# First rows of x ahead of the weights, a longer assumed time for early loads, and a new table of rules, in a planned three-part layer kernel

## The chip, the cores and the metric

The kernel runs on one core of one Trainium2 chip. The metric is the device time of one execution in microseconds (us); lower is better. A core has five engines that each work through a queue of their own in order: TensorE (PE, its weight loads PEld), VectorE (DVE), ScalarE (ACT), GpSimd (POOL) and SyncE (SP), which issues all the transfers of this kernel.

## The reference

The input x has 8 sequences of 1024 tokens with 256 channels. Four residual steps follow one another, each on the layer norm of what came before:

```
x = x + A(layernorm(x))     # A: x' + retention(x'), 4 heads, q/k width 64, v width 128, rotary, gated
x = x + F(layernorm(x))     # F: channel mix: sigmoid(xr @ W_r) * (relu(xk @ W_k)**2 @ W_v),
                            #    xr, xk mixed with the token before
x = x + Battn(layernorm(x)) # Battn: softmax attention, 16 heads of 16, a bias by relative distance
x = x + F(layernorm(x))
```

## The kernel before, in words

**The work.** Everything is done per sequence b (`for b in range(B)`). `retention(b)` handles step A in chunks of 256 tokens (`prepare`: load of the rows and their statistics; `turn_chunk`: normalising to z, transposing, and making nT, which is split into two parts so that fast matmuls keep their precision) and then blocks of 128 tokens (`queries_keys`, `values`, `gates`, `scores`, `attend`, `state`, `output`; their PSUM tiles are qps, vps, gps, aps, ops, sps, wps; the running state is S). `ffn_front` is step F (tiles ftp, kps, rps, yps). `project_b` makes queries and keys of step Battn and stores them in DRAM (stk, vd); `maxima` computes all scores once for the row maxima (PSUM tile p, maxima in pm); `weigh` computes them again (tile s), takes exponentials (e) and sums them with the values (tile acc); `back` projects (bop) and does the last step F.

**Forms of matmul.** p and s use half of the array's rows, so two matmuls, one for each of two heads, run as a pair side by side. acc uses four column strips of the array. Nearly all others use the whole array. The planner calls these forms modes.

**The order.** The program is first recorded as a list of operations (`Plan.record`), each with an engine, a planned cost, a tail (the time until its result can be used) and a target. `Plan.issue` then plays it through on a clock of its own: at each moment each engine takes, of the operations that are ready and have a free buffer, the one with the lowest key, and the instructions are written out in that order. On the chip each engine follows this written order and waits where the data is not there yet. For a load the cost is 0.4 and the tail 2.0 plus bytes/100000, in us.

**The table.** On PE the key is the target plus additions that a rule gives: `change` (a charge for changing the mode), `least` (how many PSUM slots must be free before PE changes over to p or s), `pairs` (how many sums of acc should be ready before PE changes over to them) and four offsets for other operations, p, s and acc. There are 16 rules (`RULES`). `TURNS` is a string of 122 hexadecimal digits; digit i names the rule for the i-th stretch of 20 us of the planner's clock, and the last one holds to the end:

```
rule = RULES[int(TURNS[min(int(now / STRETCH), len(TURNS) - 1)], 16)]
```

**The start.** Targets of the loads are -1.1 for the constants (cm), the norm's weights (ln) and the first weight (`split(wqk, ...)`: four loads of 128 KB, Wq and Wk in two halves; ACT casts each half and DVE subtracts the cast from it for a second part). The first sequence's `retention` starts at -1.0, and `next_ones` (Wv, Wg, wo_a) stands just after its first steps. `later()` at -0.9 loads everything else: the weights of F and of Battn, bqk, rel, the bias table, `stk` rows of statistics (two DRAM to DRAM copies of 1 MB), and small tables from which DVE works out the factors (tiles d, db, fac, then 16 times kr, each of which two stores carry to stk; kr shares five buffers with other tiles). Of equal targets the one recorded first goes first.

Of the kernel before, what the change touches and what calls it, by code (L numbers as in the profile page):

```python
# [10 lines left out]
F32 = mybir.dt.float32  # L11
# [8 lines left out]
P = 128  # L20
# [3 lines left out]
HALF = 512  # L24
# [17 lines left out]
NC, CT = 4, 2 * P  # L42
# [34 lines left out]

STRETCH = 20
TURNS = (
    "00070270877472bf8931ef967bfe1d0522ff04383dfe37be3f1f7ef668e19e9c33271224f3e73df5"  # L80
    "5663e6176b19fd77763fbb3cafd79ff9fb9bf84111"
)
SWITCH = 0.1

# [227 lines left out]
class Plan:  # L312
# [66 lines left out]
    def record(self, eng, real, method, args, kw):  # L379
        cost = kw.pop("cost", None)  # L380
        views = [a for a in list(args) + list(kw.values()) if isinstance(a, View)]
        outs = [kw[k] for k in ("out", "accum_out") if isinstance(kw.get(k), View)]
        if "out" not in kw and isinstance(args[0], View):
            outs.append(args[0])
        if method in ("matmul", "transpose"):
            out, group = outs[0].t, kw.pop("group", None)
            op = self.last
            if op is None or op.group is not group or group is None and op.out[0] is not out:
                op = self.new(eng)
                op.out, op.cost, op.group = [], 0.0, group  # L390
                self.last = op
                k, m = args[1].shape[0], 1
                for n in args[1].shape[1:]:
                    m *= n
                op.mode = ("rows" if k == 64 and m == P else "cols") if k == 64 or m == 64 else "all"
                if out.tag == "acc":
                    op.mode = "acc"
                op.late = (0.055 if method == "transpose" else 0.1) if op.mode == "all" else 0.0
            if out not in op.out:
                op.out.append(out)  # L400
            op.cost += cost
        else:
            op = self.new(eng)
            n = 1
            for v in views:
                m = 1
                for d in v.shape[1:]:
                    m *= d
                n = max(n, m)
            if method == "dma_start":  # L410
                size = 4
                for d in (args[0] if isinstance(args[0], View) else views[0]).shape:
                    size *= d
                op.cost, op.tail = 0.4, 2.0 + size / 100000.0
            else:
                op.cost = self.estimate(eng, method, n, views, {
                    **kw, "op": args[3] if len(args) > 3 else None,
                    "scalar": len(args) > 2 and isinstance(args[2], View),
                })
                op.tail = AFTER[eng]  # L420
        op.calls.append((real, method, args, kw))
        for v in views:
            if v.t.space != "in":
                self.touch(op, v, any(v is o for o in outs))
        return op
# [186 lines left out]
def layer_kernel(ctx: ExitStack, tc: tile.TileContext, ap: dict, out: bass.AP):  # L612
    nc = tc.nc
    x = ap["x"]
# [9 lines left out]
    plan = Plan(ctx, tc)  # L624
    plan.target = -1.1
    act, dve, pool, sp = (plan.engine(n, e) for n, e in (
        ("ACT", nc.scalar), ("DVE", nc.vector), ("POOL", nc.gpsimd), ("SP", nc.sync)))
    pe = plan.engine("PE", nc.tensor)

    def const(shape, name, dt=F32):  # L630
        return plan.tile(shape, dt, name, name, 1)

    def tile2k(tag, bufs=1, dt=F32):
        return plan.tile([P, HALF], dt, tag, tag, bufs)
# [37 lines left out]
    def split(w, names):  # L672
        for c in range(ND):
            t = tile2k(f"xo{c % 2}", 2)
            for s, k in enumerate(names):
                n = 2 * D // len(names)
                sp.dma_start(t[:, s * n : (s + 1) * n], ap[k][c * P : (c + 1) * P])
            act.copy(w[0][:, c], t)
            dve.tensor_tensor(w[1][:, c], t, w[0][:, c], ALU.subtract)

    split(wqk, ("a_Wq", "a_Wk"))
    wo_a = const([P, RH, D], "wo_a")
    gn = const([P, 1], "gn")
# [27 lines left out]
    def small(shape, name, bufs=2, dt=F32):  # L711
        return plan.tile(shape, dt, name, name, bufs)
# [93 lines left out]
    def power(a, n, name):  # L806

        y = small([P, n], name + "_y", 4)
        pool.tensor_tensor(y, a, mhalf[:, :n], ALU.pow)

        t = small([P, n], name + "_t", 1)
        pool.tensor_tensor(t, y, y, ALU.mult)
        pool.tensor_tensor(t, t, a, ALU.mult)
        pool.tensor_scalar(t, t, -0.5, 1.5, ALU.mult, ALU.add)
        pool.tensor_tensor(y, y, t, ALU.mult)
        return y
# [7 lines left out]
    def moments(xc, name):  # L824

        st = small([P, 2, 6], name + "_st", 1)
        mv = small([P, 2, 2], name + "_mv", 4)
        for n in range(2):
            dve.bn_stats(st[:, n, :], xc[:, n, :])
            dve.bn_aggr(mv[:, n, :], st[:, n, :])  # L830
        less = mv[:, :, 0]
        pool.tensor_scalar(less, less, -1.0, 0.0, ALU.mult, ALU.add)
        return mv
# [14 lines left out]
    def product(a, b, name):  # L848
        m = small([P, 2], name, 4)
        pool.tensor_tensor(m, a, b, ALU.mult)  # L850
        return m
# [11 lines left out]
    def rows_in(ap2, c):  # L863
        return ap2[c * CT : (c + 1) * CT, :].rearrange("(n p) d -> p n d", p=P)
# [6 lines left out]
    xc = {}  # L871


    def retention(b):
        norms = {}

        def prepare(c):

            t = tile2k("xc", 4).rearrange("p (n d) -> p n d", n=2)
            sp.dma_start(t, rows_in(x[b], c))  # L880
            xc[b, c] = t
            mv = moments(t, "a")


            a = small([P, 4], "a_a", 1)
            pool.tensor_scalar(a[:, 2:4], mv[:, :, 1], 1.0 + EPS, EPS * EPS, ALU.mult, ALU.add)
            pool.tensor_scalar(a[:, 0:2], mv[:, :, 1], 1.0, EPS, ALU.mult, ALU.add)
            rs = power(a, 4, "a")
            rs1, rz = rs[:, 0:2], rs[:, 2:4]

            s1, m1 = small([P, 2], "a_s1", 4), product(mv[:, :, 0], rs1, "a_m1")
            pool.tensor_scalar(s1, rs1, 1.0, 1.0, ALU.mult, ALU.add)
            norms[c] = mv, rz, s1, m1
# [161 lines left out]
        plan.target = b - 1.0  # L1055
        S, gT = None, None
        prepare(0)
        nTs[0] = turn_chunk(0)
        tick()
# [3 lines left out]
        tick()  # L1063
        values(0)
        prepare(1)
        tick()
        qk = turned_heads(0)
# [7 lines left out]
        for n in range(NT):  # L1075
# [18 lines left out]
            if more:  # L1094
                qk = turned_heads(n + 1)
                tick()
                gates(n + 1)
                tick()
                if n % 2 == 0 and n + 2 < NT:
                    nTs[n // 2 + 1] = turn_chunk(n // 2 + 1)  # L1100
                    if n // 2 + 2 < NC:
                        prepare(n // 2 + 2)
                    tick()
                at = scores(qk)
                tick()
# [347 lines left out]
```

## Time and profile before

| | |
|---|---|
| median of 3 runs | 2548.52 us (2542.09, 2548.52, 2551.93) |
| profiled execution | 2557.27 us, span of its instructions 2555.5 us |
| granted TensorE clock, mean | 0.992 |
| PE busy | 2476.2 us (97%), 15814 matmuls |
| DVE, ACT, POOL busy | 2107.5, 2069.9, 1589.0 us |
| DMA | 251.17 MB, mean 98 GB/s |

Busy times are of one profiled execution. A timeline line reads: start, busy time, engine, line, operation, out<-in, shape, count, and in brackets how long the engine was idle before it and what ended that. Nearly all lines carry L608, where the recorded operations are written out, so tiles tell them apart. An engine name with q (SPq) is its sequencer, which issues transfers. In the table by stretches each row gives the stretch, its length, then busy time and count for PE, PEld, DVE, ACT and POOL, the granted clock, the share of DMA time and GB/s.

### The profile page before, as it was taken

Reading aid. Unit: us, or ns where it says so; the run is one execution under the profiler, and the core shown is the slowest. Engines: PE = TensorE matmul, PEld = TensorE weight load, DVE = VectorE, ACT = ScalarE, POOL = GpSimd, SP = SyncE. Lnnn points to the kernel's source line nnn. Section 1 sums busy time; section 2 is a strip of 40 time slices with the busy share of each in tenths; the row PEclk is TensorE's granted clock in tenths of the full one; section 3 lists DMA queues with packets and bytes.
Section 4 is the critical chain, followed back from the end, with each engine's and each line's share of the span. In section 5 each row is a group of like instructions: output and inputs, shape, how many; then the busy total and the mean of one; then the engine's idle time right before and its main releaser. Section 6 shows DMA issues by size and latency. Waiting matters only on the chain.

```text
span 2555.5 us, 51508 instructions
## 1 busy us (share of the span) xinstructions
PE 2476.2 (97%) x15814; PEld 1459.8 (57%) x15814; DVE 2107.5 (82%) x6230; ACT 2069.9 (81%) x5334; POOL 1589.0 (62%) x2675
## 2 busy tenths in 40 slices
PE   5999999999999999999999999999999999999997
PEld 3887755555555555555555555555555555554555
DVE  6767998888888888988888788888888888788855
ACT  3565598888989888988888789988898888688883
POOL 2467666666756666666656576666666666666642
PEclk9999999999999999999999999999999999999999
DMA  7136322444344333332324333333233344444322
GB/s 175 42 108 150 81 58 68 130 107 112 85 106 105 84 100 101 110 98 79 92 64 119 97 107 102 94 78 109 68 94 93 102 118 115 124 115 113 93 64 72
DMA packets 252224, 251.17 MB, mean 98 GB/s; under 512 B 89042, under 2 KB 226180, under 8 KB 251924
## 3 DMA queue, kind: packets, MB, share of 16 engines
q1 hardware_dynamic: 251956, 247.89, 36.6%
q8 instruction: 132, 2.16, 0.4%
q14 instruction: 136, 1.11, 0.2%
HBM read 151.32 MB, written 98.59 MB: 98 GB/s over the span
## 4 chain that ended last, share of the span: by engine, by line
PE 79%; DVE 8%; DMA 5%; ACT 3%; POOL 2%; issue 1%; SPq 1%; POOLq 0%; DVEq 0%; ACTq 0%
PE acc L608 16%; PE p L608 10%; PE s L608 10%; PE kps L608 4%; PE wps L608 4%; PE yps L608 4%; PE rps L608 4%; PE qkp L608 3%; PE vps L608 3%; PE qps L608 3%; PE gps L608 3%; PE ops L608 3%; DVE pm L608 3%; ACT e L608 2%; PE bop L608 2%
## 5 line engine op out<-in xcount | busy, mean ns | idle before, releaser
L608 DVE TENSOR_REDUCE pm<-p 128x1 f32<-128x512 f32 (+2 forms) x2048 | 1057.2, 557 | 89.7 <-PE p L608 87.9
L608 ACT ACTIVATE e<-s 128x512 f32<-128x512 f32 (+2 forms) x2048 | 1008.0, 527 | 52.8 <-PE s L608 49.3
L608 POOL TENSOR_TENSOR e<-e,hk 128x512 f32<-128x512 f32 (+1 forms) x558 | 614.0, 1107 | 348.7 <-ACT e L608 326.9
L608 PE MATMUL acc<-e,va 128*17 128x512 f32 x4096 | 529.5, 599 | 3.7 <-ACT e L608 3.4
L608 DVE CUSTOM_DVE_ANT_0 jmax<-p,hk 128x256 bf16<-128x256 f32 (+1 forms) x1152 | 427.0, 371 | 111.8 <-PE p L608 106.6
L608 ACT COPY e<-s 128x256 f32<-128x256 f32 (+1 forms) x1116 | 400.0, 358 | 82.3 <-PE s L608 80.2
L608 PE MATMUL p<-k,q 64*128 64x512 f32 x2048 | 460.4, 438 | 5.0 <-DVE pm L608 2.8
L608 PE MATMUL s<-q,k 64*128 64x512 f32 x2048 | 456.7, 436 | 5.8 <-DVE pm L608 3.2
L608 ACT ACTIVATE e<-e 128x512 f32<-128x512 f32 (+1 forms) x576 | 336.2, 586 | 59.0 <-POOL e L608 56.1
L608 PEld LDWEIGHTS p<-k,q 64*128 64x128 f32 x2048 | 207.5, 185 | 248.4 <-ACT e L608 93.7
L608 PEld LDWEIGHTS s<-q,k 64*128 64x128 f32 x2048 | 206.0, 185 | 204.6 <-issue 69.8
L608 PEld LDWEIGHTS acc<-e,va 128*17 128x17 f32 x4096 | 77.7, 95 | 189.5 <-issue 161.6
L608 PE MATMUL kps<-xk,W_k 128*128 128x256 f32 x512 | 130.8, 399 | 10.7 <-DVE xk L608 9.7
L608 PE MATMUL rps<-W_r,xr 128*128 128x256 f32 x512 | 126.8, 390 | 3.0 <-DVE pm L608 1.8
L608 PE MATMUL yps<-W_v,xk 128*128 128x256 f32 x512 | 127.2, 392 | 1.1 <-DVE pm L608 0.5
L608 PE MATMUL wps<-wo_a,gs 128*128 128x256 f32 x512 | 125.7, 388 | 0.6 <-ACT gs L608 0.5
L608 PEld LDWEIGHTS kps<-xk,W_k 128*128 128x128 f32 x512 | 95.2, 195 | 40.7 <-issue 19.3
L608 PE MATMUL qps<-wqk,nT 128*128 128x512 f32 x384 | 106.8, 413 | 7.0 <-DVE nT L608 6.6
L608 PEld LDWEIGHTS rps<-W_r,xr 128*128 128x128 f32 x512 | 93.4, 191 | 34.5 <-DVE pm L608 5.1
L608 PEld LDWEIGHTS yps<-W_v,xk 128*128 128x128 f32 x512 | 93.6, 192 | 28.7 <-issue 12.0
L608 PEld LDWEIGHTS wps<-wo_a,gs 128*128 128x128 f32 x512 | 92.5, 190 | 26.5 <-issue 4.7
L608 POOL TENSOR_TENSOR ao_y<-ao_a,mhalf 128x4 f32<-128x4 f32 x64 | 65.7, 1026 | 66.5 <-DVE ao_a L608 65.8
(185 smaller groups left out, 4175.3 us busy)
## 6 DMA issues: line engine op xcount, KB each, us to landing
stk<-qk SPq DMA_DIRECT2D x192, 256.0 KB
hk<-ud SPq DMA_DIRECT2D x128, 256.0 KB
q<-stk SPq DMA_DIRECT2D x128, 256.0 KB
k<-stk SPq DMA_DIRECT2D x128, 256.0 KB
od<-o SPq DMA_DIRECT2D x64, 256.0 KB
vd<-vst SPq DMA_DIRECT2D x64, 136.0 KB
va<-vd SPq DMA_DIRECT2D x32, 272.0 KB
xc<-in_x SPq DMA_DIRECT2D x32, 256.0 KB
```

The lines of the kernel that those rows point to most:

```text
L608: getattr(real, method)(*[be(a) for a in args], **{k: be(a) for k, a in kw.items()})
```

## The change

Three edits. The load of the first 256 rows of x (256 KB) is recorded before the first weight's loads, at target -1.1, into the same kind of buffer (xc) that `prepare` took before, and `prepare` of the first chunk uses it. The tail of a transfer that is recorded at a target below -0.85 becomes 2.0 plus bytes/50000 in the planner's clock; this takes in all loads and stores of the start, the first two chunks of x and everything in `later`. The string `TURNS` is replaced; 22 of its 122 digits are the same at the same place.

```diff
 TURNS = (
-    "00070270877472bf8931ef967bfe1d0522ff04383dfe37be3f1f7ef668e19e9c33271224f3e73df5"
-    "5663e6176b19fd77763fbb3cafd79ff9fb9bf84111"
+    "01f23221077472bf8958e587083491e68871f2b49d36a6f05684487b6ccde338cff55263777f276f"
+    "53f68b29ff7a5356f4326638b8f59ba679b7155111"
 )
...
-                op.cost, op.tail = 0.4, 2.0 + size / 100000.0
+                op.cost, op.tail = 0.4, 2.0 + size / (50000.0 if self.target < -0.85 else 100000.0)
...
+    first = plan.tile([P, HALF], F32, "xc", "xc", 4)
+    sp.dma_start(
+        first.rearrange("p (n d) -> p n d", n=2), x[0][:CT, :].rearrange("(n p) d -> p n d", p=P)
+    )
     split(wqk, ("a_Wq", "a_Wk"))
...
-            t = tile2k("xc", 4).rearrange("p (n d) -> p n d", n=2)
-            sp.dma_start(t, rows_in(x[b], c))
+            t = (first if b == c == 0 else tile2k("xc", 4)).rearrange("p (n d) -> p n d", n=2)
+            if b or c:
+                sp.dma_start(t, rows_in(x[b], c))
```

## The prediction

> **What bounds the kernel now.** First the page: busy times and the chain that ended last.
>
> ```profile
> span 2555.5 us, 51508 instructions
> ...
> PE 2476.2 (97%) x15814; PEld 1459.8 (57%) x15814; DVE 2107.5 (82%) x6230; ACT 2069.9 (81%) x5334; POOL 1589.0 (62%) x2675
> ...
> PE 79%; DVE 8%; DMA 5%; ACT 3%; POOL 2%; issue 1%; SPq 1%; POOLq 0%; DVEq 0%; ACTq 0%
> ```
>
> TensorE sets the end; only 79 us of the span are without a matmul. The table of busy times by 80 us stretches tells where these lie (second number: PE busy).
>
> ```profile
> 0.00:80.00 80.00, 48.31 (x272) 36.08 (x273) 52.34 (x120) 35.81 (x76) 26.11 (x79) 0.96 0.58 140
> ...
> 2480.00:2555.00 75.00, 61.64 (x310) 42.80 (x302) 39.20 (x91) 32.68 (x69) 24.03 (x59) 0.95 0.24 72
> sum 2555.00, PE 2476.16 PEld 1459.77 DVE 2107.54 ACT 2069.91 POOL 1588.98; mean PE 77.38 PEld 45.62 DVE 65.86 ACT 64.68 POOL 49.66
> ```
>
> PE is idle for 31.7 us in the first 80 us, 13.4 us in the last 75, and 33.8 us in all the 2400 us between. So a better start is worth at most about 30 us. The timeline of the start shows what it waits for.
>
> ```profile
> 3.60 0.43 SPq L608 DMA_DIRECT2D xc<-in_x  x1
> ...
> 9.33 0.75 DVE L608 BATCH_NORM_STATS2 a_st<-xc 128x6 f32<-128x256 f32 x2 [1.33 <-DMA xc<-in_x]
> ...
> 15.49 0.62 ACT L608 CAST wg_a<-xo 128x512 fp32r<-128x512 f32 x1 [4.16 <-DMA xo<-in_a_Wg]
> ...
> 17.36 1.09 ACT L608 ACTIVATE z<-xc,a_nb,a_y 128x256 f32<-128x256 f32 x2
> ...
> 26.49 0.16 DVE L608 TENSOR_TENSOR d<-d,d 16x16 f32<-16x16 f32 x1 [6.09 <-DMA d<-in_b_rel]
> ...
> 29.59 0.67 DVE L608 TENSOR_TENSOR nT<-z,nT 128x512 fp32r<-128x512 f32 x1
> 30.31 2.21 PEld L608 LDWEIGHTS qps<-wqk,nT 128*128 128x128 f32 x6 [7.88 <-DVE nT L608]
> ```
>
> The first rows land at 9.33, but the first real matmul (qps) runs at 30.31. It waits for one subtraction (nT) whose inputs ACT had ready at 22.4. That subtraction stands in VectorE's queue behind an instruction on a table of bias differences, d, whose 1 KB load landed only at 26.49. So the first rows' load is not the last thing that the start waits for. A second stall follows, again in VectorE's queue.
>
> ```profile
> 49.80 0.74 DVE L608 TENSOR_SCALAR kr<-stat,fac 16x1024 f32<-16x1024 f32 x1 [0.84 <-DMA stk<-kr]
> ...
> 51.43 1.23 PE L608 MATMUL ops<-S,qkT 64*128 64x128 f32 x8 [5.25 <-ACT S L608]
> ```
>
> Here the state S sits behind kr, which waits until an earlier kr has been stored. Last, PE in the steady part, where the table of rules works.
>
> ```profile
> 1000.60 1.91 PE L608 MATMUL acc<-e,va 128*17 128x512 f32 x16
> 1002.44 0.50 PE L608 MATMUL s<-q,k 64*128 64x512 f32 x2
> ...
> 1005.29 0.50 PE L608 MATMUL p<-k,q 64*128 64x512 f32 x2
> 1005.63 0.39 PE L608 MATMUL s<-q,k 64*128 64x512 f32 x2
> 1005.86 0.39 PE L608 MATMUL p<-k,q 64*128 64x512 f32 x2
> 1006.18 1.05 PE L608 MATMUL acc<-e,va 128*17 128x512 f32 x8
> 1007.16 1.99 PE L608 MATMUL wps<-wo_a,gs 128*128 128x256 f32 x8
> ```
>
> Read the starts. Three pairs of score matmuls (half the array's rows each) take 0.89 us before acc begins; the step between the later pairs is 0.23, so a run costs 3 x 0.23 and about 0.20 once. Over the whole trace, runs of one, two and three pairs take 0.430, 0.662 and 0.895 us (medians): 0.198 per run and 0.2325 per pair. For acc, 16 matmuls take 1.84 and 8 take 0.98: 0.86 per eight and 0.12 per run. I count 873 runs of row pairs and 429 of acc, so 173 + 54 = 227 us go to changes of form that PE's busy time does not show as idle. This is what the table can move: 64 runs of pairs more or fewer are 12.7 us, 0.5% of the time and about what a measurement of this kernel can tell from no change.
>
> **The first load moved up.** No instruction, byte or buffer is added; one load goes from seventh to third in SP's queue and passes four weight loads of 128 KB. It would issue at 1.70 instead of 3.60 (third place), and four weight loads issue 0.47 us later each. What follows goes by the order of VectorE's queue, which the planner writes out by its own clock; I work that clock by hand, for order only. Before, the second weight's correction ends at 7.01 there, x is due at 7.42. Now the four weight loads are due at 6.62 and 7.42, the correction runs 8.12 to 8.72, x is due at 8.44: the statistics again stand behind the correction. On the chip the second weight is now the seventh load; if that place still lands near 9.3, its cast (0.62) and correction (0.69) put the statistics at 10.6, 1.3 us later than before, though x lies there by about 5.4 (the landing of the fourth load before). The other end, if the weights land at once after x, is 1 us earlier than 9.33.
>
> **The doubled cost of early loads.** It changes only order. By my hand count the second gate weight's casts fall behind z on ACT: GpSimd's chain takes 5.3 us from the statistics to the last factor (9.33 to 14.62), so z comes at 15.9 instead of 17.36 and nT's inputs about 21 instead of 22.4. On SP, W_g waits for a buffer that frees later by that clock, so wo_b, bqk, rel, bv and bo pass it, and wq and c_hot (0.30 MB) fall behind the two d loads. SP also shows a second rule: each load starts when the one eight places earlier has landed (the 15th at 9.32 on the 7th, the 18th at 12.12 on the 10th, the 27th at 16.83 on the 19th), so being two places earlier helps d. With 0.30 MB less ahead, at 140 to 340 GB/s in those slices, d lands 1 to 2 us earlier: 25.0. On VectorE d still precedes nT by the planner's clock (13.6 against 17.9), with room for four kr (0.7 each, all its buffers) instead of two: +1.4. So nT goes at 29.59 - 1.5 + 1.4 = 29.5: no gain. Bounds: 4 us earlier if d is freed earlier still, 2 later if not at all. For the stall on S: stores of kr are now thought 3.3 instead of 2.65 us long, so more of the retention's work comes between the kr; this is worth between 0 and the 5.3 us shown, and could cost as much as one more kr wait (0.8 to 2). I take 2.5. Start in all: -2.5, from -9 to +4.
>
> The Trainium skill speaks against the doubling: DMA: Bandwidth & Descriptors, section Anatomy of one DMA, fits one transfer (on the GpSimd path) as 2.0 us plus bytes over 436 GB/s. As an estimate by that page, 256 KB would take 2.6 us, shorter than the old guess of 4.6, and d would land 6 us earlier in both kernels. The row decides: x issued at 3.60 was used at 9.33, 5.7 us, between the old 4.6 and the new 7.2.
>
> **The table.** It changes 100 of 122 entries and so nearly the whole order of PE after the start. Its effect on runs can be bounded from the trace: I counted runs of pairs in each 20 us stretch, took the mean for each rule (6.0 to 8.4, all near 7.3) and weighted the new counts of rules against the old. That gives +5 runs, +1 us. A chance order moves this by more: 5% of the runs is 44 x 0.198 = 8.7 us, and a third of the idle 33.8 us is 11 us, either way; together 14. The end of the program (13.4 us idle) waits on the last batch's own chain, which no edit touches: nothing, or 4 us either way if other work is left over for it.
>
> **Sum.** The profiled execution took 2557.27 us (span 2555.5 and 1.8 around it): -2.5 + 1 gives 2555.8. The median of the runs shown is 2548.52, 8.75 below that execution; on that scale 2547.0.
>
> **The rivals.** *The start really shortens* (faster): nT passes d's chain on VectorE, qps starts at 22 instead of 30.3 (-8), and the wait on S goes (-5.3): 2548.5 - 13.3 + 1 = 2536. For it: the only cause of the late nT is a queue order. Against it: the planner's clock keeps 4 us between the two. *Fewer runs* (faster): 80 runs less are 15.8 us, 2531. For it: 227 us of changes. Against it: the mix of rules is the same. *More runs* (slower): score pairs go in shorter runs, because slots in PSUM come free at other times; each extra run costs 0.198 us in the steady part, and from 64 extra runs (7%) it decides; 85 give 16.8, with the start's 2.5 back 2563. For it: new rules forbid short runs less (58 entries with a charge of 0.1 or more for a change of form, before 67). Against it: the means by rule. *The early load does nothing* is part of my forecast.
>
> **How the numbers follow.** No measurable change 0.50, at 2547 (its own range 2536 to 2561); the shorter start 0.12; fewer runs 0.16; more runs 0.22. Faster by over 0.5% 0.28, slower by over 0.5% 0.22. The range takes the +-14 of the table and the start's -9 and +4, cut to leave 2 in 10 outside: 2525 to 2566.
>
> **What would show it.** Right: x third on SP at 1.7, yet its statistics at 10 to 11; z before the gate weights' casts; nT behind d and four kr, qps at 28 to 31; runs of pairs between 830 and 917; PE idle 27 to 32 us in the first 80. Wrong: qps by 24, over 64 runs of difference, or idle in the middle beyond 34 +- 11 us.

## The result, and the profile after

| | before | changed |
|---|---|---|
| median of 20 runs each, us | 2549.15 (2542.09 to 2552.81) | 2554.36 (2548.56 to 2559.59) |
| ratio | | 1.0018, 95% interval 1.0011 to 1.0025 |
| profiled execution (its span), us | 2557.27 (2555.5) | 2553.84 (2552.1) |

By the ratio the changed kernel is slower by 4.6 us, with an interval of 2.8 to 6.4 (the medians differ by 5.2). That lies in the predicted range and inside the 0.5% band, but the sign is the opposite of the predicted -1.5. The two spans point the other way: the one execution of before that was profiled was longer than all of its 20 timed runs, so a comparison of span with span misleads here. Stretches and distances within the traces are used below instead.

The page of the changed kernel has nearly the same busy times as before.

```profile
span 2552.1 us, 51521 instructions
...
PE 2472.3 (97%) x15814; PEld 1459.4 (57%) x15814; DVE 2102.6 (82%) x6230; ACT 2069.4 (81%) x5334; POOL 1590.3 (62%) x2675
...
PE 83%; DVE 6%; DMA 5%; ACT 3%; POOL 1%; issue 1%; SPq 1%; POOLq 0%; DVEq 0%; ACTq 0%
```

The table by stretches of 80 us (second number: PE busy) shows where a difference lies:

```profile
0.00:80.00 80.00, 46.25 (x264) 35.37 (x265) 49.98 (x117) 34.77 (x75) 25.72 (x78) 0.96 0.55 140
...
sum 2552.00, PE 2472.26 PEld 1459.38 DVE 2102.61 ACT 2069.41 POOL 1590.27; mean PE 77.26 PEld 45.61 DVE 65.71 ACT 64.67 POOL 49.70
```

PE does 46.25 us of work in the first 80 us, where before did 48.31: idle 33.75 instead of 31.7. The timeline of the start tells why.

```profile
1.70 0.43 SPq L608 DMA_DIRECT2D xc<-in_x  x1
...
8.41 0.74 DVE L608 BATCH_NORM_STATS2 a_st<-xc 128x6 f32<-128x256 f32 x2
...
12.99 1.09 ACT L608 ACTIVATE z<-xc,a_nb,a_y 128x256 f32<-128x256 f32 x2 [2.41 <-POOL a_nb L608]
...
23.94 0.17 DVE L608 TENSOR_TENSOR d<-d,d 16x16 f32<-16x16 f32 x1 [6.64 <-DMA d<-in_b_rel]
24.03 0.41 DVE L608 TENSOR_SCALAR W_v<-W_v 128x512 f32<-128x512 f32 x1
...
25.46 0.74 DVE L608 TENSOR_SCALAR kr<-stat,fac 16x1024 f32<-16x1024 f32 x1
26.13 0.40 DVE L608 TENSOR_TENSOR ob<-ob,bps 1x256 f32<-1x256 f32 x1
...
26.46 1.40 DVE L608 TENSOR_SCALAR kr<-stat,fac 16x1024 f32<-16x1024 f32 x2
...
27.79 0.73 DVE L608 TENSOR_SCALAR wo_a<-wo_a,gn 128x1024 f32<-128x1024 f32 x1
28.45 0.73 DVE L608 TENSOR_SCALAR kr<-stat,fac 16x1024 f32<-16x1024 f32 x1
29.11 0.67 DVE L608 TENSOR_TENSOR nT<-z,nT 128x512 fp32r<-128x512 f32 x1
...
46.14 1.16 PE L608 MATMUL ops<-vs,at 128*128 128x128 f32 x8 [1.34 <-POOL at L608]
...
50.15 1.16 PE L608 MATMUL ops<-vs,at 128*128 128x128 f32 x8 [1.26 <-POOL at L608]
...
53.96 2.90 PE L608 MATMUL qps<-wqk,nT 128*128 128x512 f32 x6 [2.65 <-DVE nT L608]
```

The load is third on SP, and the statistics come 0.9 us earlier than in before's profile, z 4.4 us earlier. The 0.9 is chance: in the eight profiles of this study with the load in its old place and the old start the statistics begin at 7.50 to 9.33 (mean 8.1), in the eleven with the changed start at 8.41 to 9.04 (mean 8.7). The row at 8.41 shows no idle time before it: VectorE was still at the second weight's correction. And nT still stands behind d, and now behind four kr, the scalings of W_v and wo_a and the sum for ob. From d to nT it takes 5.17 us (23.94 to 29.11); before it took 3.10 (26.49 to 29.59). In place of PE's one wait on S (5.25) there are three, 1.34 and 1.26 on at (the masked scores, from GpSimd) and 2.65 on the second nT.

When d lands varies between executions, so each distance is given from d on. The table puts together what the profiles of this study show; "old start" are before and three runs below that keep VectorE's order of its start, "changed start" are the changed kernel four times and two runs that have its start.

| us | old start, 4 profiles | changed start, 6 profiles |
|---|---|---|
| d starts, mean (least to most) | 25.88 (25.29 to 26.49) | 25.45 (23.94 to 26.93) |
| d to first nT | 3.10 in all | 5.17 or 5.18 in all |
| PE work in the first 80 us | 48.9 | 44.8 |
| start of the 600th matmul | 129.7 | 132.8 |
| d to 600th matmul | 103.8 (103.16 to 105.03) | 107.3 (106.33 to 108.74) |

Over the whole span PE is idle for 78.45 us on the mean of the four and for 83.19 on the mean of the six. Of these 4.7 us, 4.1 lie in the first 80; the sum of PE's busy time differs by 1.3 the other way.

### The profile page after: what moved, and what is told of

Same layout as the page of the kernel before. It is cut to its first block, busy times and chain, and to the rows that moved or that the text cites. A ratio compares the mean times of both kernels' runs of the same rounds, so it can differ in the third digit from the quotient of the medians.

```text
span 2552.1 us, 51521 instructions
## 1 busy us (share of the span) xinstructions
PE 2472.3 (97%) x15814; PEld 1459.4 (57%) x15814; DVE 2102.6 (82%) x6230; ACT 2069.4 (81%) x5334; POOL 1590.3 (62%) x2675
## 4 chain that ended last, share of the span: by engine, by line
PE 83%; DVE 6%; DMA 5%; ACT 3%; POOL 1%; issue 1%; SPq 1%; POOLq 0%; DVEq 0%; ACTq 0%
PE acc L608 17%; PE p L608 11%; PE s L608 11%; PE yps L608 5%; PE kps L608 4%; PE wps L608 4%; PE qps L608 4%; PE rps L608 4%; PE vps L608 3%; PE qkp L608 3%; PE ops L608 3%; PE gps L608 3%; DVE pm L608 2%; ACT e L608 2%; PE bop L608 2%; PE bvp L608 2%
## 5 line engine op out<-in xcount | busy, mean ns | idle before, releaser
L608 PE MATMUL acc<-e,va 128*17 128x512 f32 x4096 | 522.4, 597 | 1.0 <-ACT e L608 1.0
L608 PE MATMUL vps<-wv_a,nT 128*128 128x512 f32 x384 | 106.9, 415 | 0.5 <-ACT e L608 0.3
```

Of the source, the lines that this page charges most:

```text
L608: getattr(real, method)(*[be(a) for a in args], **{k: be(a) for k, a in kw.items()})
```

## The experiments

All kernels but the two on the table alone and the controls write out an order that was planned beforehand, so only the named part differs. Ratios are to before on the same chip, with 95% intervals.

### Which half: the start or the rest

```diff
-order = planned(changed)
+order = planned(changed)[up to 60 us of the planner's clock] + the rest in planned(before)'s order   # first and third run
+order = planned(before)[up to 60 us] + the rest in planned(changed)'s order                          # second and fourth
```

> The written order of the changed kernel for everything that its planner writes in its first 60 us, then the order of the kernel before. Theory S (the 5 us are lost at the start: PE was idle for 33.8 us instead of 31.7 in the first 80): slower than before by 2 to 5 us. Theory R (they are lost in the order of the rest, which the new table sets): within 1.5 us of before.

> The opposite splice: the start of the kernel before, then the changed kernel's order. Theory S: within 1.5 us of before. Theory R: slower than before by 3 to 6 us, about as the changed kernel is (5.2).

> The same kernel as e1, on another chip and beside the changed kernel, to halve the uncertainty: theory S (start) 2 to 5 us slower than before, theory R (rest) within 1.5.

> The same kernel as e2, to halve its uncertainty: slower than before by 1 to 3 us if the start has most of the loss (4.6 and 5.0 in e1 and e7), by 3 to 5 if it has half of it.

> The changed kernel itself beside e5 to e7 on one chip: 3.5 to 6.5 us slower than before, as measured already.

Changed start with the old rest: 1.0018 (1.0007 to 1.0030) and, on another chip, 1.0023 (1.0010 to 1.0035). Old start with the new rest: 1.0009 (1.0000 to 1.0018) and 1.0006 (0.9995 to 1.0017). The changed kernel itself, again: 1.0033 (1.0020 to 1.0046). So the start alone costs about 0.2%, 5 us. The new rest costs between nothing and 4.6 us; these runs can't tell more.

### The early load alone

```diff
 SP: constants, norm weights, first half of Wq,
+    first rows of x,
     second half of Wq, Wk, ...
-    first rows of x, ...
```

> The kernel before with one instruction moved: the load of the first rows of x issues third on SP instead of seventh; nothing else differs. If the early load is worth nothing, as predicted, because its statistics stand behind the second weight's correction on VectorE and nT behind the bias table: the time within 1 us of before, qps at 30 to 31. If the first rows were the bound: qps earlier by 2 us or more and the time with it. If the later weights hurt: statistics at 10.6 instead of 9.3 and qps unchanged.

1.0000 (0.9992 to 1.0009); d at 25.78, nT at 28.88, 3.10 after d as before. By itself the load's place is worth nothing that shows, within about 2 us.

### The table alone

```diff
-TURNS = new            # first run: changed kernel, planned anew with the old table
+TURNS = old
-TURNS = old            # second run: kernel before, planned anew with the new table
+TURNS = new
```

> The changed kernel with the old table of rules (the planner then writes its order anew). Runs of row pairs in the written order 878 (before 873, changed 883), runs of full-array work 598 (577, 575), in all 1955 (1934, 1928). If the table is only right for the start it was found with: slower than the changed kernel by about 2 us from those runs (23 x 0.09 - 5 x 0.2 + 8 x 0.12) and than before by 5 to 9. If the new table itself is what costs: faster than the changed kernel.

> The kernel before with the new table alone. Runs in all 1995 (before 1934): full-array 622 instead of 577, row pairs 891 instead of 873: 45 x 0.09 + 18 x 0.2 = 7.7 us slower than before, if runs set the time of the steady part. If the table's order does not matter: within 2 us of before.

Changed start with the old table: 2626.12 us, 1.0301 (1.0288 to 1.0314). Old start with the new table: 2658.11 us, 1.0424 (1.0411 to 1.0438). With a start whose planned times are only a few us off, the old table loses 75 us. The page of the run with the changed start and the old table:

```profile
span 2626.6 us, 51456 instructions
...
PE 2520.8 (96%) x15814; PEld 1473.2 (56%) x15814; DVE 2107.8 (80%) x6230; ACT 2071.3 (79%) x5334; POOL 1591.8 (61%) x2675
...
L608 PE MATMUL acc<-e,va 128*17 128x512 f32 x4096 | 540.7, 602 | 4.2 <-ACT e L608 3.4
```

and of the run with the old start and the new table:

```profile
span 2656.2 us, 51507 instructions
...
PE 2531.6 (95%) x15814; PEld 1473.3 (55%) x15814; DVE 2109.9 (79%) x6230; ACT 2072.0 (78%) x5334; POOL 1589.9 (60%) x2675
```

Against the kernel with the same start and its own table, PE is busy 48.5 and 55.4 us longer with the same 15814 matmuls, and idle 26 and 45 us longer. The changes of form don't explain it: the written orders have 1955 runs of one form (changed: 1928) and 1995 (before: 1934), by the prediction's 0.198 us each 5 and 12 us at most. What makes the same matmuls take 2% longer in PE's busy time was not settled. What is settled is that a table belongs to the start with which it was found.

### The stretch from d to the first nT

```diff
 VectorE, changed kernel: d, W_v, fac ...,
+    nT,                                     # fourth run: nT ahead of all six
     kr, ob, kr, kr, wo_a,
+    nT,                                     # first and second run: nT passes one kr
     kr,
-    nT,
     ...
     S, gs,
+    second nT,                              # second run only
     kr, gs, kr, kr, ss, kr, ...
-    second nT,
```

> The changed kernel's written order with one instruction of VectorE moved: the first nT stands behind the factors (fac) and ahead of the first four kr, ob and wo_a instead of behind them. In the changed kernel these six take 3.66 us (25.46 to 29.11). Theory (what stands between d and the first nT on VectorE is the step that cost the time): nT comes 1.5 us after d instead of 5.2, the first qps 3.6 earlier, PE does 3 to 4 us more work in the first 80 us (48 to 49 instead of 44.9 on the mean), and the kernel is 3 to 5 us faster than the changed one (the control of this call), level with before. Rival (the other waits of the start, on at and on the second nT, hold the loss): qps 3.6 earlier, but the first 80 us keep 45 us of PE work and the time stays within 1.5 us of the changed kernel's.

> As the run with the first nT moved, and also the second nT (at 53.15 in the changed kernel) ahead of the five kr, the products with ops and the statistics that stand between S and it on VectorE; its inputs are there at about 45.8. Theory: the first move alone gives back 3 to 4 us; the second takes away the wait of 2.65 us that qps shows at 53.96, so 2 us more in the first 80 us (50 to 51 of PE work) and up to 2 us in the time. Rival (the second and the at waits hold the loss): only this run is 3 to 5 us faster than the changed kernel, the first move is not. A third outcome, no gain from either, would say that the order on VectorE between 25 and 55 us is not the cause.

> The changed kernel as it is, for comparison on the same chip: both theories expect 1.002 to 1.003 of before, first qps between 29.8 and 32.6, PE work in the first 80 us between 43 and 47.

1.0024 (1.0013 to 1.0034) and 1.0017 (1.0006 to 1.0027), the control 1.0019 (1.0010 to 1.0029): no gain from either. The first edit was weaker than meant: in the written order nT's inputs are not there any earlier, so it passed only one kr, and d to nT is still 4.52 us. The second run's 600th matmul comes 105.8 us after d, 1.5 less than the mean of the changed start, but its time shows nothing of that. The next three runs go further: the fourth run of the diff, the same stretch put into the kernel before, and the control.

```diff
 VectorE, kernel before:
-    W_v, wo_a, ob,                          # each at its own place ahead of d
     d,
+    W_v,
     fac ..., kr,
-    copy of ups,
+    ob, kr,
     kr,
+    wo_a, kr,
     nT,
+    copy of ups,
-    kr, kr,
     ...
```

> The changed kernel with the first nT on VectorE right behind the factors, ahead of four kr, ob and wo_a; all other engines' orders are as in the changed kernel. (In the run e13 it passed only one kr, 0.65 us.) By theory one (what stands between d and the first nT costs the time) nT comes 1.5 us after d instead of 5.2, and all that follows is 3.7 us earlier: 3 to 4 us more PE work in the first 80 us, 600th matmul 104.5 us after d instead of 108.3, time 3 to 4 us below the changed control. By theory two (VectorE as a whole is the bound from d on: what nT passes comes behind it and ahead of ta, and in the changed kernel VectorE idles only 1.16 us ahead of ta) qps is 3.7 earlier but ta at most 1.2; the 600th matmul 107 to 108.3 after d, and the time within 1.5 us of the control.

> The kernel before with VectorE's order between d and the first nT as in the changed kernel: W_v, ob, wo_a and two more kr ahead of nT, the copy of ups behind it; all other engines' orders as before. nT 5.17 us after d instead of 3.10 (both theories). Theory one: all that follows is 2.07 later, the 600th matmul 105.5 us after d instead of 103.5, the time 2 us above before. Theory two: the two kr only change places with nT, but W_v, ob and wo_a (1.33) are new work behind d, so ta is 1.3 to 2.1 later and the 600th matmul 104.8 to 105.5 after d; the time 1 to 2 us above before. A time equal to before's and a 600th matmul 103.5 after d would say that neither holds, and that a later wait hides it.

> The changed kernel as it is, on the same chip: 1.0015 to 1.003 of before, the first nT 5.2 us after d, the 600th matmul 108 to 109 us after d.

Without the stretch the changed kernel takes 1.0004 of before (0.9995 to 1.0013); with it, the control, 1.0024 (1.0015 to 1.0034). The intervals don't meet: with nT ahead of that work, what the start costs is gone. The move is 3.75 us, though, and the change had added only 2.07. Its timeline (ta is VectorE's first instruction on the result of qps):

```profile
24.26 0.16 DVE L716 TENSOR_TENSOR d<-d,d 16x16 f32<-16x16 f32 x1 [7.44 <-DMA d<-in_b_rel]
...
25.68 0.67 DVE L716 TENSOR_TENSOR nT<-z,nT 128x512 fp32r<-128x512 f32 x1
...
26.41 2.93 PE L716 MATMUL qps<-wqk,nT 128*128 128x512 f32 x6 [8.42 <-DVE nT L716]
...
31.79 0.67 DVE L716 TENSOR_TENSOR ta<-qps,cm 128x512 f32<-128x512 f32 x1
...
42.64 1.16 PE L716 MATMUL ops<-vs,at 128*128 128x128 f32 x8 [0.50 <-POOL at L716]
```

nT is 1.42 us after d, 3.75 sooner than in the changed kernel, and ta 7.53 after d instead of 8.86: 1.3 of the 3.75 got past VectorE's queue at ta. But the wait on at shrinks from 1.34 to 0.50 too, and the 600th matmul is 104.5 us after d instead of 107.3 on the mean, or 106.4 in the control (where 108 to 109 was expected). That is between what the two theories expected (3.7 and at most 1.2), with PE at 49.66 us of work in the first 80.

Put into the kernel before, the stretch moves its start as theory one said, and as the upper end of theory two:

```profile
25.89 0.16 DVE L725 TENSOR_TENSOR d<-d,d 16x16 f32<-16x16 f32 x1 [8.19 <-DMA d<-in_b_rel]
...
31.06 0.67 DVE L725 TENSOR_TENSOR nT<-z,nT 128x512 fp32r<-128x512 f32 x1
...
34.75 0.69 DVE L725 TENSOR_TENSOR ta<-qps,cm 128x512 f32<-128x512 f32 x1 [1.95 <-PE qps L725]
```

nT 5.17 after d, ta 8.86 (before 6.79), the 600th matmul 105.9 (old start's four: 103.8), PE work in the first 80 us 46.84 (48.9). So the added 2.07 shifts the start by 2.1, about half of what the changed start loses there. The time, 1.0006 (0.9996 to 1.0016), has room for the 2 us and for nothing; alone it would prove little.

### d's load, and the kr elsewhere

```diff
 SP, kernel before:
+    stat, far, two loads of d,
     copy of 1 MB (stk), wq, c_hot, copy of 1 MB (stk),
-    stat, far, two loads of d,
```

> The kernel before with only SP's order changed: the four small loads for the bias table (stat, far and the two d) issue ahead of the two 1 MB copies into stk instead of behind them. If d is late because of those copies: d's first instruction on VectorE at 17.5 to 19 instead of 26.5, nT behind the copy of ups at about 24.4 and qps at 25 instead of 30.3; the later kr still wait for their stores, so 2 to 5 us faster. If d is late for its own latency or its place among the eight loads in flight: qps at 29 or later and no change.

0.9993 (0.9982 to 1.0004). The 1 KB of d had stood behind two copies of 1 MB and, between them, the loads of wq and c_hot; the run passes all four and doesn't tell them apart:

```profile
19.74 0.16 DVE L714 TENSOR_TENSOR d<-d,d 16x16 f32<-16x16 f32 x1
...
26.07 0.67 DVE L714 TENSOR_TENSOR nT<-z,nT 128x512 fp32r<-128x512 f32 x1
...
40.98 1.40 DVE L714 TENSOR_SCALAR kr<-stat,fac 16x1024 f32<-16x1024 f32 x2 [0.96 <-DMA stk<-kr]
```

d is 6.75 us earlier than in before's profile (its load is issued 3.07 earlier, 15.40 instead of 18.47, and used 4.3 us later instead of 8.0), nT 3.5 (it stood behind the copy of ups, which had to wait until 24.94), the 600th matmul 2.6; in the time no more than a hint of it.

```diff
 VectorE, kernel before:
-    d ... fac, 16 kr between 26 and 56 us
+    d ... fac from 40 us and a kr every 4 us of the planner's clock     # first run
+    d ... fac and 16 kr in VectorE's idle gaps between 126 and 186 us   # second; third: with the changed start as well
```

> The kernel before, with the bias table's instructions on VectorE (the d chain and the 16 kr) and their stores put later in the written order: the chain at 40 us of the planner's clock, a kr every 4 us from there. PE, ACT and GpSimd keep their order exactly. If the queue order on VectorE is what holds the start, as the reading of the trace says: qps at about 24.5 instead of 30.3, no wait for S at 51, PE idle in the first 80 us 18 to 24 instead of 31.7, and 6 to 12 us faster. If the loads or ACT bind as well: less than 3 us.

> As e4, but the 16 kr and the d chain stand where VectorE waited in the kernel before between 126 and 186 us (gaps of 0.7 to 3.0 us there). In e4's profile PE was 9 us ahead at its 100th matmul and 2 ahead at its 600th, because the later kr lengthened the retention's chain of dependences at 45 to 116 us. If that is where e4's lead went: PE 5 to 9 us ahead of the kernel before at its 600th matmul, and 4 to 8 us faster. If the lead is lost whatever VectorE does (the first sequence's chain waits on itself until PE has other work): 2 us ahead at most, and the time within 2 us of before.

> The changed kernel's start (first 60 us of the planner's clock) and the rest of the kernel before, with kr and the d chain moved as in e5. The early rows of x and the gate weights' casts behind z now have a free VectorE queue: if they are worth something once the queue does not hold nT, qps at 20 to 22 (e4: 24.6) and 2 to 4 us faster than e5. If not: as e5.

Every 4 us: 1.0006 (0.9996 to 1.0016). nT came at 23.84, and PE led by 9 us at the 100th matmul but by 1.9 at the 600th. The chain of waits of that run shows the kr in it:

```profile
95.99 0.63 ACT qk L722
96.68 0.57 issue
97.67 0.65 DVE kr L722
99.10 0.70 DVE ss L722
100.06 1.02 POOL ao_y L722
```

Between 95 and 120 us this chain through VectorE and GpSimd, and not PE, carries the end, and each kr stands in it with 0.65. The next run bears this out: with the kr out of that stretch PE's lead at the 600th matmul is 10.8 us.

In the gaps: 0.9991 (0.9982 to 1.0000) with the old start; with the changed one 0.9980 (0.9969 to 0.9990), 2548.59 us against 2553.45 of before and 2560.54 of the changed kernel on the same chip. This version beats both. It also bears on the cause: with d and kr out of the way the changed start costs nothing against the old one (0.9980 and 0.9991), so what it costs lies in VectorE's queue with them. Its start:

```profile
13.18 1.09 ACT L733 ACTIVATE z<-xc,a_nb,a_y 128x256 f32<-128x256 f32 x2 [2.16 <-POOL a_nb L733]
...
15.92 1.86 PE L733 MATMUL bps<-wo_b,bv 128*1 128x256 f32 x4 [15.92 <-DMA bv<-in_b_bv]
...
17.71 1.12 PE L733 MATMUL ntp<-cm,z 128*128 128x128 f32 x4
...
18.26 0.73 DVE L733 TENSOR_SCALAR wo_a<-wo_a,gn 128x1024 f32<-128x1024 f32 x1
...
20.83 0.69 DVE L733 TENSOR_TENSOR nT<-z,nT 128x512 fp32r<-128x512 f32 x1 [1.84 <-ACT z L733]
...
21.58 2.20 PEld L733 LDWEIGHTS qps<-wqk,nT 128*128 128x128 f32 x6 [3.15 <-DVE nT L733]
```

nT is at 20.83, with the old start at 24.00, where it stood behind the copy of ups (23.52). It now waits for its inputs, but not for x: ACT had normalised the rows by 14.3, and their transposition (ntp) stood on PE behind bps, which waited for the load of bv until 15.92. So in no run did the early load count. Against before's trace PE leads by 13.0 us at the 600th matmul and by 6.0 at the 1500th (with the old start by 10.8 and 5.7); in the times 4.9 us are left of it (2.5). Where the rest goes between 130 and 270 us was not settled.

## Why the prediction was right and wrong

**The first load moved up: right in worth and in its first reason.** It was forecast as nothing, since the statistics stand behind the second weight's correction and nT in VectorE's queue, and alone it is nothing (1.0000). The times of the hand count were off: statistics at 8.41 instead of 10.6, z at 12.99 instead of 15.9. z is early mostly because the casts of the gate weight went behind it on ACT, as forecast. Neither is of use while nT stands behind d, and without d the transposition stands behind bps.

**The step that failed: "d lands 1 to 2 us earlier: 25.0", "instead of two: +1.4" and with them "no gain".** The mechanism was right and two terms were mis-sized. d comes 0.4 us earlier on the mean, not 1.5. What stands between d and nT grew by 2.07, not 1.4: beside the two kr (1.33) also W_v, ob and wo_a came behind d (0.22, 0.33 and 0.66 by the starts of the lines; W_v partly fills a pause), and only the copy of ups (0.47) left the stretch: 2.07 in all. The prediction followed the longer tail for SP and for kr, and not for every VectorE instruction whose own load is now thought longer; that this tail is why the planner put the three there is read from the code and was not tried by itself. So nT is 1.6 us later on the mean instead of level. That nT's place decides is shown by the runs with it ahead of the stretch and behind it, 1.0004 against 1.0024; the added 2.07 alone moved the start of the kernel before by 2.1, with no loss of time clear of noise (1.0006).

**The second failed term: the stall on S, "I take 2.5".** The wait on S did go. But PE waits 1.34 and 1.26 for at and 2.65 for the second nT: 5.25 in sum, as much as the one wait had been. The credit was for a wait by its name. The 2.65 end with VectorE's queue again, which had as many kr to do; the two on at end with GpSimd, and why they came was not tried. Together the start puts the 600th matmul 3.1 us later (3.5 counted from d), where the forecast had 2.5 earlier, and PE does 4.1 us less in the first 80 us. That is most of the 4.6 in the time; about half of it goes by the 2.07, and how the other half divides among these waits stays open.

**The doubling.** The page DMA: Bandwidth & Descriptors of the Trainium skill (section Anatomy of one DMA), weighed in the prediction, would have both guesses too long for 256 KB: by its fit, as an estimate, 2.6 us. No run here priced the load alone: in the changed kernel x is used 6.7 us after its issue (1.70 to 8.41), but VectorE was at work until then, so this only bounds it from above.

**The table: right in outcome, wrong in reason.** The forecast +1 +- 14 held (old start with new rest: 1.0009 and 1.0006), and so did the bounds on runs: 883 of pairs, by the written order, against 873. But the rule that a table's worth can be had from counting runs of pairs fell: tables exchanged alone cost 75 and 107 us, of which runs of one form make 5 and 12 at most. So the outcome was luck as far as this reason goes. (A slip in the sum before it: 429 runs of acc at 0.12 are 51 us, not 54, which changes nothing.) "More runs" as the slower rival had the wrong price; had the table not been found anew with its start, a loss of 3% was waiting, well outside the predicted range.

**The idle time.** 33.75 us in the first 80, outside the forecast 27 to 32; in the middle 32.5, within 33.8 +- 11. The first is the line of the profile that speaks against the step that failed.

## What to carry to other kernels

Ask of a load that is moved up not when its data lands but what else its consumer's engine has in its queue by then, and cost every instruction there, those too whose own loads the change delays. A wait that goes by name can come back under another name if the work in front of it is still done: count the engine's work from one landing to the next, and move that work into measured gaps of the engine (here 12 us better than the changed kernel), but not into a stretch where a dependence chain runs through that engine. An order and the table that was tuned on it are one object; exchange one half of them alone and the loss can be twenty times what the change itself is worth.

## What the runs showed of the hardware

The granted clock fell after pauses of PE of 1 to 3 us. In the changed kernel without the stretch PE pauses 1.25 us before ops (46.65) and 2.86 before qps (50.67), with work between; the table of stretches shows the granted clock (third number from the end):

```profile
45.00:50.00 5.00, 1.56 (x14) 1.17 (x12) 4.87 (x11) 1.57 (x5) 2.24 (x3) 0.86 0.81 146
50.00:55.00 5.00, 4.33 (x10) 3.47 (x11) 4.37 (x11) 0.00 (x0) 3.58 (x8) 0.50 0.93 248
55.00:60.00 5.00, 5.00 (x27) 4.20 (x26) 3.84 (x10) 2.40 (x6) 3.28 (x12) 0.96 0.19 68
```

The shares below 1.00 add up to 0.7 + 2.5 + 0.2 = 3.4 us lost, that is 6.8 us at half speed, and the records of the granted clock show it as one stretch at half speed from 48.6 on. In the changed kernel itself single pauses were followed by the same: 1.92 us without a matmul from 616.3, and half speed for 3.4 us from 618.9; 2.34 us from 211.4, and half speed for 3.4 us from 216.1. In the kernel before it was 6.8 us from 1222.6 after a pause of 1.33 at 1220.0, and nothing after one of 1.36 at 1758.4. The page TensorE: Matmul & The Clock Gate of the Trainium skill (section Part 1: The HAM clock gate) puts the fall behind an idle window of about 3.4 us; in these traces pauses of 1.3 to 2.3 us were enough, though not each time. So a wait of 2 us can cost 1.7 or 3.4 more, half of the 3.4 or 6.8 at half speed.

And a small load can be late by the company it is in: d, 1 KB, was used at 26.49 behind two copies of 1 MB and two smaller loads, and at 19.74 ahead of them and issued 3.07 earlier. With the same written order it came anywhere from 23.94 to 26.93 in six profiles of the changed start, which alone moves the start by 3 us from one execution to the next.
